# Attention scores from single-pass products of split operands, in batches of six blocks

## The chip, the cores and the metric

The kernel runs on one core of one Trainium2 chip. The metric is the time on the device in microseconds (us); lower is better. A core has a matrix engine (TensorE, PE in the profile, its weight loads PEld), VectorE (DVE), ScalarE (ACT), GpSimd (POOL) and SyncE (SP), whose queue issues most of the DMAs here. Matrix products are written to PSUM; everything else is kept in SBUF.

## The reference

The input has 4 images of 384 channels and 48 x 48 positions, so N = 2304 positions an image. There are 8 heads of 48 channels.

```python
x_flat = x.reshape(B, C, N).transpose(0, 2, 1)
local = depthwise_conv_7x7(x) * inv + shift              # batch norm folded in
x_norm = layernorm(x_flat)
q, k, v = split_heads(x_norm @ qkv_w.T + qkv_b)
q = q + split_heads(layernorm(local_flat))
attn = softmax(einsum('bhnd,bhmd->bhnm', q, k) * hd ** -0.5)
out = einsum('bhnm,bhmd->bhnd', attn, v)
out = x_flat + merge_heads(out) @ proj_w.T + proj_b
```

All of it is in float32.

## The kernel before

**Tiling.** An image is cut into 6 groups of 384 positions (`G`), 8 rows of the picture each, so there are 24 query groups, numbered `t`. Heads go in 4 pairs `p`. In the packed layout the first head of a pair has partitions 0 to 47, the second 64 to 111; the last pair's channels lie as "tails" of 16 rows at 48 to 63 and 112 to 127 of the other three, and `gather_tails` collects them by DMA into tiles of their own (`kt` for keys, `qt` for queries).

**Stages.** A start-up stage loads and scales the weights and makes keys, values and queries of image 0 (`from_x`, one call a group of positions). Then, for each of the 24 query groups, attention runs in 12 slots of 6 key blocks (a block is 128 keys), three slots a head pair. Before groups 6, 12 and 18 there is a key stage for the next image, six calls of `from_x`, each with three projections for values, keys and queries and, for the image that has just ended, the output. `both` takes one step of two such projections.

**Attention.** `score` makes the scores of a block for the two heads of a pair, transposed: keys along partitions, 384 queries along the free dimension. It issues four matmuls, each with 48 rows and 64 columns of the array: two heads by two halves of the block's keys. ScalarE then exponentiates the whole block in one instruction of 128 x 768 (L803) into a tile `pt`. `weigh` multiplies a block that is two older (`LAG`) with the values, again in four matmuls, 64 x 64 of the array: two halves of the keys by two heads. The values carry a column of ones, so that the sums of the softmax come with it. The sums stay in PSUM over all 18 blocks of a pair. `score` and `weigh` take turns on TensorE. After a pair's end `pair_out` copies one half of the sums on ScalarE and `pair_add` adds the other on VectorE.

**PSUM.** There are two pools of two slots each, `ring` for the scores and `accumulator` for the sums, every slot of two banks. Other stages take from both in turn (`two_banks`).

**VectorE's work.** The 7x7 convolution is done tap by tap on VectorE: 147 steps a group (L280, L284), each a multiply and add over about 384 elements. It runs as a stream through all groups. `plan` gives every half slot a number of steps: it has a room in us for each point (`spare`, `spare_at_keys`) and dues, by which the convolution of group t+1 must be complete (slot 8 of group 0, slot 6 of the others). `convolve` issues the share of a point. Norms (`Norm`), `local_end` and `query_end` (the queries of group t+1, in slot 10) and the division of the previous group's outputs are put at fixed slots.

**Order.** PE, DVE and ACT run in the order in which the code is written; the same holds for each DMA queue. SP's queue waits in order too, so a DMA whose data are late holds back those after it.

Of the kernel before, what the change touches and what calls it, by code (L numbers as in the profile page):

```python
# [10 lines left out]
F32 = mybir.dt.float32  # L11
AF = mybir.ActivationFunctionType
# [3 lines left out]
P = 128  # L16
# [12 lines left out]
LAG = 2  # L29
# [16 lines left out]
def unshifted_pass(  # L46
# [35 lines left out]
    ps_r = ctx.enter_context(tc.tile_pool(name="ps_r", bufs=2, space=bass.MemoryType.PSUM))  # L82
    ps_o = ctx.enter_context(tc.tile_pool(name="ps_o", bufs=2, space=bass.MemoryType.PSUM))
# [3 lines left out]
    def ring():  # L87
        return ps_r.tile([P, 2, 512], F32, tag="r", name="r")

    def accumulator():  # L90
        return ps_o.tile([P, 2, 512], F32, tag="o", name="o")


    either = cycle((accumulator, ring))

    def two_banks():
        return next(either)()
# [39 lines left out]
    natural = const.tile([P, CC, T0 + 1], F32, tag="natural", name="natural")  # L137
# [20 lines left out]
    taps_in = big.tile([P, CC, T0], F32, tag="kt0", name="taps_in")  # L158
# [28 lines left out]
    packing = big.tile([P, len(pairs), P], F32, tag="k1", name="packing")  # L187
# [14 lines left out]
    def pack():  # L202
# [21 lines left out]
    staged = [  # L224
        big.tile([P, CC, C], F32, tag=f"k{NG - 1 - i}", name=f"staged{i}") for i in range(3)
    ]
# [84 lines left out]
    def spare(t, s, half):  # L311
        b, g = divmod(t, NG)
        first, second = norm_slots(t)
        time = 3.8 - (0.7 if s % 3 == 0 and half else 0.0)
# [18 lines left out]
    def spare_at_keys(b, g, h):  # L333
        time = 4.6 - {0: 0.6, 4: 1.2}.get(h, 0.0)
        if g < later(b):
            time -= {0: 2.3, 2: 2.2, 4: 2.3}.get(h, 0.0)
        if 0 < g <= later(b):
            time -= {1: 0.4, 3: 2.6}.get(h, 0.0)
        return time - {(1, 1): 2.7, (2, 1): 1.4}.get((g, h), 0.0)
# [36 lines left out]
    class Norm:  # L376
# [37 lines left out]
        def mean_kept(self):  # L414

            m = ring()[:, 0, :G]
# [88 lines left out]
    def gather_tails(dst, src):  # L505

        for c in range(CC):
            for r in (0, 64):
                nc.sync.dma_start(
                    out=dst[r + 16 * c : r + 16 * c + 16], in_=src[r + HD : r + 64, c, :]  # L510
                )

    keys, values = {}, {}

    def from_x(b, g, before=None, ao=None):
# [3 lines left out]
        k = big.tile([P, CC, G], F32, tag=f"k{g}", name=f"k{b}_{g}")  # L519
        k3 = big.tile([P, G], F32, tag=f"kt{g}", name=f"kt{b}_{g}")  # L520

        flat = big.tile([P, NB * NH * HA + 64 - HA], F32, tag=f"v{g}", name=f"v{b}_{g}")
        v = flat[:, 0 : NB * NH * HA].rearrange("p (t h d) -> p t h d", t=NB, h=NH)
        keys[b, g], values[b, g] = (k, k3), flat
# [14 lines left out]
        def key(u, r):  # L539
            project(r[:, :G], lambda c: w_qk[:, c, 1, u, :], lambda c: src[:, c, :])  # L540
            yield
            nc.scalar.activation(
                k[:, u, :], r[:, :G], AF.Identity, bias=qkb[:, 1, u : u + 1]
            )
            if u == CC - 1:
                gather_tails(k3, k)
# [107 lines left out]
    def output_bias():  # L654

        m = ring()[:, 0, 0:CC]
# [17 lines left out]
    def query_end(t):  # L674
# [3 lines left out]
        q3 = work.tile([P, G], F32, tag="qt", name=f"qt{t}")  # L678
# [6 lines left out]

    outputs = {}

    ended = []

    def pair_out():  # L690
# [3 lines left out]
        t, p, sums = ended[0]  # L694
# [9 lines left out]
    def pair_add():  # L704

        if not ended:
            return
        t, p, sums = ended.pop()
        ao, ao3, den = outputs[t]
        dst = (ao[:, p, :] if p < CC else ao3)[0 : 64 + HA]  # L710
        nc.vector.tensor_add(dst, sums[0 : 64 + HA, 1, :G], dst)  # L711
# [34 lines left out]
    def load_residual(t, tag="xr", bufs=2):  # L746
# [13 lines left out]
    def fetch(t):  # L760
        if t < NT - NG:
            ao = work.tile([P, CC, G], F32, tag="af", name=f"af{t}")
# [21 lines left out]
    sums = None  # L784

    def score(t, p, kb):
        q, q3 = queries[t]
        k, k3 = keys[t // NG, kb // NB]
        blk = kb % NB
        r = ring()  # L790
        for j in range(2):
            rows = slice(64 * j, 64 * j + HD)
            kk, qq = (k[rows, p, :], q[rows, p, :]) if p < CC else (k3[rows], q3[rows])
            for h in halves:
                nc.tensor.matmul(  # L795
                    r[h, j, :G],
                    lhsT=kk[:, blk * P + h.start : blk * P + h.stop],
                    rhs=qq,
                    start=True,
                    stop=True,  # L800
# [4 lines left out]
        if jobs:  # L805
            jobs.popleft()()

    def weigh():
        nonlocal sums
        t, p, kb, pt = weighing.popleft()  # L810
        if kb == 0:
            sums = accumulator()
        for i, h in enumerate(halves):
            for j in range(2):
                first = (kb % NB * NH + 2 * p + j) * HA
                nc.tensor.matmul(  # L816
                    sums[halves[j], i, :G],
                    lhsT=values[t // NG, kb // NB][h, first : first + 64],
                    rhs=pt[h, j, :],
                    start=kb == 0,  # L820
                    stop=kb == KB - 1,
                )
        if kb == KB - 1:
            ended.append((t, p, sums))

    def attend(t, s, half):

        p, k0 = s // (KB // BATCH), s % (KB // BATCH) * BATCH
        n = BATCH // 2
        for kb in range(k0 + n * half, k0 + n * half + n):  # L830
            score(t, p, kb)
            if len(weighing) > LAG:
                weigh()

    def rest():
        while weighing:
            weigh()
        while jobs:
            jobs.popleft()()

# [71 lines left out]
    both(making)  # L912
    convolve_first(7)
    for g in range(1, NG):
# [28 lines left out]
        both(making)  # L943
        if not last:
            convolve_first(7)
    query_end(0)
    nc.vector.tensor_add(pb, pb, added)
    plan(n_first - (each - PE_TAPS))

    for t in range(NT):  # L950
        b, g = divmod(t, NG)
        if g == 0 and b:

            rest()
            pair_out()
            pair_add()
# [678 lines left out]
```

## Time and profile before

| | us |
|---|---|
| device time, median of 3 runs | 2856.93 |
| lowest and highest run | 2855.59, 2859.35 |
| span of the profiled execution | 2857.6 |
| TensorE busy | 2838.7 (99%) |
| VectorE busy | 2344.6 (82%) |
| ScalarE busy | 1649.5 (58%) |
| start-up, to the first score | 144.3 |
| each of three key stages | 140.4 |
| last outputs, after the last group | 41.5 |

The page gives the profiled execution as its span, first to last instruction, and the span lies within the three runs, so nothing is added to it. A page line reads: line of the code, engine, operation, tile written <- tiles read, partitions x elements, count, then busy us and mean ns of one, then the engine's idle time before it and what ended that. Matmuls that run abreast in parts of the array overlap, so their count times their mean is more than their busy time. A float32 matmul has two records here, each with a weight load of its own. In the tables of windows, each engine's busy time in a stretch is followed by its number of instructions.

### The profile page before, as it was taken

To read this page: it belongs to the slowest core of one execution; us is meant where nothing else is said; L and a number is where in the kernel's file an instruction comes from. 1 tells how busy PE (TensorE), PEld (TensorE's weight loads), DVE (VectorE), ACT (ScalarE), POOL (GpSimd) and SP (SyncE) were. 2 spreads that over 40 slices of the span, in tenths; PEclk is the share of its full clock that TensorE was granted. 3 is DMA by queue.
4 is the path that set the end of the run, shared out by engine and by line. 5 is a ranking of instruction groups with operands and counts; after the bars stand their busy time and mean duration, and the time that the engine had idled before them with its cause. 6 is when DMAs were issued, how large, how long until landed. Compare 5 with 4: busy or idle time off the path is not lost.

```text
span 2857.6 us, 70328 instructions
## 1 busy us (share of the span) xinstructions
PE 2838.7 (99%) x29558; PEld 1778.1 (62%) x29558; DVE 2344.6 (82%) x4635; ACT 1649.5 (58%) x2350; POOL 14.9 (1%) x77
## 2 busy tenths in 40 slices
PE   9999999999999999999999999999999999999999
PEld 5544444654554466666655546888875545788886
DVE  7899999999888988878888889887788787887401
ACT  4366666666226666666622666666652366666662
POOL 1000000000000000000000000000000000000000
PEclk9999999999999999999999999999999999999999
DMA  5101121112231211121132112101113211111111
GB/s 106 40 5 36 45 49 35 36 26 43 71 83 25 46 35 41 31 39 24 38 94 70 28 30 50 36 22 37 44 25 94 53 20 29 43 23 32 46 38 63
DMA packets 103433, 123.71 MB, mean 43 GB/s; under 512 B 43136, under 2 KB 89152, under 8 KB 103104
## 3 DMA queue, kind: packets, MB, share of 16 engines
q1 hardware_dynamic: 99568, 115.48, 17.0%
q8 instruction: 234, 3.83, 0.6%
q10 hardware_dynamic: 2992, 3.62, 0.4%
q14 instruction: 95, 0.78, 0.1%
q0 software_dynamic: 544, 0.01, 0.0%
HBM read 81.39 MB, written 27.03 MB: 38 GB/s over the span
## 4 chain that ended last, share of the span: by engine, by line
PE 92%; DVE 6%; DMA 0%; POOL 0%; ACT 0%; issue 0%; DVEq 0%; ACTq 0%; POOLq 0%
PE o L816 37%; PE r L795 37%; PE o L503 9%; PE r L503 9%; DVE acc L284 5%; DMA pb<-in_proj_b_dram 0%; PE r L299 0%; PE r L412 0%; ACT pt L803 0%; DVE sq L401 0%; DVE xn L681 0%; DMA parts<-part 0%; DVE sq L400 0%; POOL qk_vec L167 0%; DVE acc L672 0%
## 5 line engine op out<-in xcount | busy, mean ns | idle before, releaser
L803 ACT ACTIVATE pt<-r 128x768 f32<-128x768 f32 x1728 | 1399.6, 810 | 760.1 <-PE r L795 743.6
L284 DVE SCALAR_TENSOR_TENSOR acc<-slab,vec,acc 128x368 f32<-128x368 f32 (+6 forms) x3447 | 1756.3, 582 | 1.2
L816 PE MATMUL o<-pt,v 64*64 64x384 f32 x13824 | 1544.7, 483 | 0.0
L795 PE MATMUL r<-xn,k 48*64 48x384 f32 x10368 | 1157.8, 483 | 3.7 <-ACT pt L803 3.7
L816 PEld LDWEIGHTS o<-pt,v 64*64 64x64 f32 x13824 | 715.3, 133 | 406.7 <-issue 224.0
L795 PEld LDWEIGHTS r<-xn,k 48*64 48x64 f32 x10368 | 531.9, 133 | 316.2 <-issue 176.1
L795 PE MATMUL r<-qt,kt 48*64 48x384 f32 x3456 | 388.1, 482 | 0.1
L795 PEld LDWEIGHTS r<-qt,kt 48*64 48x64 f32 x3456 | 181.3, 133 | 99.1 <-issue 43.8
L711 DVE TENSOR_TENSOR ao<-o,ao 113x384 f32<-113x384 f32 x72 | 39.9, 554 | 194.0 <-PE r L795 176.8
L503 PE MATMUL o<-xn,w_qk 128*128 128x384 f32 x450 | 153.3, 486 | 0.0
L503 PE MATMUL r<-xn,w_qk 128*128 128x384 f32 x414 | 141.1, 486 | 0.0
L503 PEld LDWEIGHTS o<-xn,w_qk 128*128 128x128 f32 x450 | 85.5, 190 | 59.6
L503 PEld LDWEIGHTS r<-xn,w_qk 128*128 128x128 f32 x414 | 78.7, 190 | 54.8
L536 ACT COPY v<-r 128x384 f32<-128x384 f32 x42 | 18.2, 482 | 126.9 <-PE r L503 126.9
L503 PE MATMUL r<-w_v,xn 128*128 128x384 f32 x252 | 85.2, 487 | 0.0
L711 DVE TENSOR_TENSOR aot<-o,aot 113x384 f32<-113x384 f32 x24 | 13.3, 556 | 82.4 <-ACT aot L702 64.8
L503 PE MATMUL o<-af,w_o 128*128 128x384 f32 x222 | 75.0, 487 | 0.0
L400 DVE TENSOR_TENSOR sq<-sq 128x384 f32<-128x384 f32 x47 | 26.0, 554 | 57.7 <-ACT sq L395 56.2
L503 PEld LDWEIGHTS r<-w_v,xn 128*128 128x128 f32 x252 | 47.6, 190 | 34.4 <-issue 1.8
L503 PE MATMUL o<-w_v,xn 128*128 128x384 f32 x180 | 64.4, 498 | 1.3 <-ACT w_v L635 1.3
L503 PEld LDWEIGHTS o<-af,w_o 128*128 128x128 f32 x222 | 42.1, 190 | 29.2
L771 DVE SCALAR_TENSOR_TENSOR xr<-r,pb,xr 128x384 f32<-128x384 f32 x27 | 16.4, 617 | 51.8 <-ACT xn L555 41.9
(139 smaller groups left out, 1036.9 us busy)
## 6 DMA issues: line engine op xcount, KB each, us to landing
xr<-in_x_dram SPq DMA_DIRECT2D x24, 576.0 KB
slab<-in_x_dram SPq DMA_DIRECT2D x32, 378.0 KB
held<-ao SPq DMA_DIRECT2D x20, 576.0 KB
af<-held SPq DMA_DIRECT2D x20, 576.0 KB
rb<-rden SPq DMA_DIRECT2D x48, 216.0 KB
out_dram<-xr SPq DMA_DIRECT2D x54, 192.0 KB
xn<-in_x_dram SPq DMA_DIRECT2D x46, 216.0 KB
slab<-in_x_dram SPq DMA_DIRECT2D x14, 297.0 KB
```

Of the source, the lines that this page charges most:

```text
L284: nc.vector.scalar_tensor_tensor(dst, src, weight, dst, ALU.mult, ALU.add)
L400: nc.vector.tensor_add(self.buf[:, 0, :], src[:, 0, :], src[:, 1, :])
L503: nc.tensor.matmul(dst, lhsT=weights(c), rhs=src(c), start=c == 0, stop=c == CC - 1)
L536: nc.scalar.copy(v[:, blk, :, 0:HD], r[:, :C].rearrange("p (h d) -> p h d", d=HD))
L711: nc.vector.tensor_add(dst, sums[0 : 64 + HA, 1, :G], dst)
L771: nc.vector.scalar_tensor_tensor(xr[:, co, :], m, pb[:, co : co + 1], xr[:, co, :], ALU.add, ALU.add)
L795: nc.tensor.matmul(r[h, j, :G], lhsT=kk[:, blk * P + h.start : blk * P + h.stop], rhs=qq, start=True, stop=True,)
L803: nc.scalar.activation(pt, r[:, :, :G], AF.Exp, scale=SCALE)
L816: nc.tensor.matmul(sums[halves[j], i, :G], lhsT=values[t // NG, kb // NB][h, first : first + 64], rhs=pt[h, j, :], start=kb == 0, stop=kb ...
```

## The change

- The keys and queries are split into a high part, rounded on writing to `float32r`, and a low part, the remainder. Since a head has 48 rows and a half of the array 64, parts are stacked along rows: the first stationary tile has the 48 high rows of the keys and the first 16 low ones, the second the other 32 low rows twice. Three queries tiles stand against them (high; low; the rest of high and of low), and a block's scores are the sum of three matmuls a head, each 64 rows by 128 columns in `float32r`, accumulated in PSUM.
- Six blocks of scores are issued, then the six blocks of values. The values use 128 rows by 64 columns, in float32 as before. The sums are taken out of PSUM after every six blocks (`sums_out`) and added up in SBUF (`sums_add`).
- PSUM is one pool of four slots for everything.
- The split keys are written to DRAM (`keys_out`), and a pair's stacked keys are read from it (`stack_keys`, two buffers), at the beginning of the pair before. The stacked queries are made by a ScalarE copy (`high_queries`), a VectorE subtraction and DMAs within SBUF (`low_queries`), in the second slot of the pair before.
- The rooms of the plan are given new values. Start-up tiles, residuals and fetched outputs get other buffers.

The core of the diff:

```diff
+HALF = mybir.dt.float32r
-LAG = 2
...
-    ps_r = ctx.enter_context(tc.tile_pool(name="ps_r", bufs=2, space=bass.MemoryType.PSUM))
-    ps_o = ctx.enter_context(tc.tile_pool(name="ps_o", bufs=2, space=bass.MemoryType.PSUM))
+    ps = ctx.enter_context(tc.tile_pool(name="ps", bufs=4, space=bass.MemoryType.PSUM))
...
-        time = 3.8 - (0.7 if s % 3 == 0 and half else 0.0)
+        time = 3.6 - (0.0 if half else 0.6) - (0.6 if half and s % 3 == 1 else 0.0)
...
-        time = 4.6 - {0: 0.6, 4: 1.2}.get(h, 0.0)
+        time = 4.6 - {0: 0.6, 1: 0.7, 2: 1.4, 4: 1.2}.get(h, 0.0)
...
     def gather_tails(dst, src):
-        for c in range(CC):
+        for i, c in enumerate((*range(CC), 0)):
...
+    def keys_out(b, g, u, k):
+        at = slice(g * G, (g + 1) * G)
+        for j in range(2):
+            r = 64 * j
+            for head, rows, n in (
+                (2 * u + j, slice(0, HD), (r, r + HD)),
+                (6 + j, slice(16 * u, 16 * u + 16), (r + HD, r + 64)),
+            ):
+                nc.sync.dma_start(
+                    out=keys[b][head, rows, :, at], in_=k[n[0] : n[1]].bitcast(F32)
+                )
+    def stack_keys(b, p, at=slice(0, N)):
+        if at.start == 0:
+            stacks[b, p] = big.tile([P, 2, N], HALF, tag="ks", name=f"ks{b}_{p}", bufs=2)
+        dst = stacks[b, p].bitcast(F32)
+        for j in range(2):
+            r, head = 64 * j, keys[b][2 * p + j]
+            nc.sync.dma_start(out=dst[r : r + HD, 0, at], in_=head[:, 0, at])
+            nc.sync.dma_start(out=dst[r + HD : r + 64, 0, at], in_=head[0:16, 1, at])
+            for i in range(2):
+                nc.sync.dma_start(
+                    out=dst[r + 32 * i : r + 32 * i + 32, 1, at], in_=head[16:HD, 1, at]
+                )
...
-            nc.scalar.activation(
-                k[:, u, :], r[:, :G], AF.Identity, bias=qkb[:, 1, u : u + 1]
-            )
-            if u == CC - 1:
-                gather_tails(k3, k)
+            bias = qkb[:, 1, u : u + 1]
+            k = work.tile([P, 2, G], HALF, tag="pt", name=f"k{b}_{g}_{u}", bufs=5)
+            nc.scalar.activation(k[:, 0, :], r[:, :G], AF.Identity, bias=bias)
+            nc.vector.scalar_tensor_tensor(
+                k[:, 1, :], r[:, :G], bias, k[:, 0, :], ALU.add, ALU.subtract
+            )
+            keys_out(b, g, u, k)
...
+    def high_queries(t, p):
+        qs = work.tile([P, 3, G], HALF, tag="qs", name=f"qs{t}_{p}", bufs=5)
+        stacked[t, p] = qs
+        nc.scalar.copy(qs[:, 0, :], query_of(t, p))
+    def low_queries(t, p):
+        qs = stacked[t, p]
+        nc.vector.tensor_sub(qs[:, 1, :], query_of(t, p), qs[:, 0, :])
+        qs = qs.bitcast(F32)
+        for j in range(2):
+            r = 64 * j
+            if p < CC:
+                nc.sync.dma_start(out=qs[r + HD : r + 64, 0:2], in_=qs[r : r + 16, 0:2])
+            for i in range(2):
+                nc.sync.dma_start(
+                    out=qs[r + 32 * i : r + 32 * i + 32, 2], in_=qs[r + 16 : r + HD, i]
+                )
...
+    def sums_out():
...
+        t, p, i, sums = ended.pop()
+        if i:
+            part = work.tile([P, G], F32, tag="part_o", name=f"o{t}_{p}_{i}")
+            nc.scalar.copy(part[0 : 64 + HA], sums[0 : 64 + HA, 0, :G])
+            parts_of.append((t, p, i, part))
+            return
...
+    def sums_add():
...
+        nc.vector.tensor_add(dst, dst, part[0 : 64 + HA])
...
     def score(t, p, kb):
-        r = ring()
-        for j in range(2):
-            rows = slice(64 * j, 64 * j + HD)
-            kk, qq = (k[rows, p, :], q[rows, p, :]) if p < CC else (k3[rows], q3[rows])
-            for h in halves:
-                nc.tensor.matmul(r[h, j, :G],
-                    lhsT=kk[:, blk * P + h.start : blk * P + h.stop], rhs=qq, start=True, stop=True)
+        ks, qs = stacks[t // NG, p], stacked[t, p]
+        r = two_banks()
+        for i, (w, m) in enumerate(((0, 0), (0, 1), (1, 2))):
+            for j, rows in enumerate(halves):
+                nc.tensor.matmul(r[:, j, :G],
+                    lhsT=ks[rows, w, kb * P : (kb + 1) * P], rhs=qs[rows, m, :],
+                    start=i == 0, stop=i == 2)
...
-    def weigh():
-        for i, h in enumerate(halves):
-            for j in range(2):
-                nc.tensor.matmul(sums[halves[j], i, :G],
-                    lhsT=values[t // NG, kb // NB][h, first : first + 64], rhs=pt[h, j, :],
-                    start=kb == 0, stop=kb == KB - 1)
+    def weigh(i, sums):
+        for j in range(2):
+            nc.tensor.matmul(sums[halves[j], 0, :G],
+                lhsT=values[t // NG, kb // NB][:, first : first + 64], rhs=pt[:, j, :],
+                start=i == 0, stop=i == BATCH - 1)
...
                 both(making)
+                stack_keys(b, 0, slice(gk * G, (gk + 1) * G))
+                if gk == NG - 2:
+                    high_queries(t, 0)
+                if gk == NG - 1:
+                    low_queries(t, 0)
...
         for s in range(NSLOT):
-            attend(t, s, 0)
+            score_batch(t, s)
+            pair, third = divmod(s, KB // BATCH)
+            if third == 0:
+                if pair < NP - 1:
+                    stack_keys(b, pair + 1)
+                elif g < NG - 1:
+                    stack_keys(b, 0)
+            if third == 1 and pair < NP - 1:
+                high_queries(t, pair + 1)
...
                 if g < NG - 1:
                     query_end(t + 1)
+                    high_queries(t + 1, 0)
...
             convolve("slot", t, s, 0)
+            sums_add()
-            attend(t, s, 1)
...
+            weigh_batch(t, s)
             convolve("slot", t, s, 1)
+            if third == 1 and pair < NP - 1:
+                low_queries(t, pair + 1)
+            if following and s == second + 1 and g < NG - 1:
+                low_queries(t + 1, 0)
```

## The prediction

> **What bounds the kernel now.** I read the page from the top: the engines' busy time, the forty slices, then the costliest groups.
>
> ```profile
> PE 2838.7 (99%) x29558; PEld 1778.1 (62%) x29558; DVE 2344.6 (82%) x4635; ACT 1649.5 (58%) x2350; POOL 14.9 (1%) x77
> ...
> PE   9999999999999999999999999999999999999999
> ...
> DVE  7899999999888988878888889887788787887401
> ```
> TensorE is never idle, but VectorE reads 9 for the first quarter too: two engines are full there.
>
> ```profile
> L803 ACT ACTIVATE pt<-r 128x768 f32<-128x768 f32 x1728 | 1399.6, 810 | 760.1 <-PE r L795 743.6
> L284 DVE SCALAR_TENSOR_TENSOR acc<-slab,vec,acc 128x368 f32<-128x368 f32 (+6 forms) x3447 | 1756.3, 582 | 1.2
> L816 PE MATMUL o<-pt,v 64*64 64x384 f32 x13824 | 1544.7, 483 | 0.0
> L795 PE MATMUL r<-xn,k 48*64 48x384 f32 x10368 | 1157.8, 483 | 3.7 <-ACT pt L803 3.7
> ```
> There are 1728 blocks (24 query groups x 4 head pairs x 18). Scores (L795) and values (L816) have 8 records a block each; they run four abreast, so durations may not be added. The timeline gives the pace, with the change of array shape into the key stage below it:
>
> ```profile
> 1004.59 0.85 PE L795 MATMUL r<-xn,k 48*64 48x384 f32 x8
> 1005.23 0.85 PE L816 MATMUL o<-pt,v 64*64 64x384 f32 x8
> 1005.88 0.85 PE L795 MATMUL r<-xn,k 48*64 48x384 f32 x8
> ```
> ```profile
> 717.87 0.50 PE L816 MATMUL o<-pt,v 64*64 64x384 f32 x4
> 718.30 0.59 PE L503 MATMUL r<-w_v,xn 128*128 128x384 f32 x1
> ```
> A block takes 1.29 us, 0.645 for scores and as much for values; a slot of six takes 7.76. The second fence: starts 0.43 apart instead of 0.32, and the first matmul 0.10 longer than the usual 0.49, so a change of shape costs 0.15 to 0.2. Last, the windows by query group (us, then busy us of PE, PEld, DVE, ACT, POOL, clock, DMA share, GB/s):
>
> ```profile
> 144.30:246.20 101.90, 97.61 (x1141) 44.17 (x1144) 100.82 (x194) 63.06 (x85) 0.00 (x0) 0.97 0.10 19
> 246.20:343.80 97.60, 95.05 (x1156) 46.80 (x1152) 96.85 (x190) 61.22 (x83) 0.00 (x0) 0.98 0.17 41
> 343.80:437.00 93.20, 93.20 (x1156) 44.97 (x1152) 92.61 (x182) 61.53 (x83) 0.00 (x0) 1.00 0.17 40
> ...
> 717.40:857.80 140.40, 140.40 (x445) 82.29 (x440) 122.18 (x236) 34.47 (x71) 0.16 (x2) 1.00 0.29 79
> ...
> 1043.40:1136.70 93.30, 93.30 (x1158) 64.31 (x1154) 81.70 (x160) 61.52 (x83) 0.00 (x0) 1.00 0.14 35
> ```
> In the first image VectorE is 99% busy and sets the end of the first two groups; from the second image on it has 12 us of room in a group. A key stage (717 to 858) is TensorE's.
>
> **What the Trainium skill says.** "FP8 and Floating Point Precision", TensorE Precision Notes: true FP32 takes four passes (high and low parts against each other), reduced FP32 is read and truncated. The trace agrees with four passes: 1.29 us for two rounds of four is 0.162 us a pass. It shows no reduced product. "TensorEngine Tiling (Array Packing)", Key Properties: changing the tiling mode drains the engine; the trace has that at 0.15 to 0.2 us. "TensorE: Matmul & The Clock Gate", LDWEIGHTS: a load takes its columns over 1.2 GHz, whatever the rows, so an estimated 107 ns for 128 columns. The trace agrees: the first 128x128 matmul above waits 0.10 us.
>
> **The change, part by part.**
> *Scores.* A block's four 48x64 four-pass matmuls become six 64x128 single-pass ones, two row halves abreast and three deep: 3 x 0.162 = 0.485 us instead of 0.645. The unknown is the pass. Bounds: 0.162 (one column a cycle, as each pass of the four) and 0.323 (half that rate); less than a pass is excluded. I take 0.162, since a load of 0.105 fits beneath it.
> *Values.* Two 128x64 matmuls of four passes abreast instead of four 64x64: 0.645 again.
> *Batching.* Two changes of shape a slot, which today's order has none of: 0.35 us. Slot: 18 x 0.162 + 24 x 0.162 + 0.35 = 7.15 us. ScalarE starts exponentials 0.70 us apart when they queue (two in 1.51 us at 858.76), so six end about 5.2 us after the first score and the last values wait for none; of four PSUM slots, the one for the sums waits for the third exponential, within 0.1 us of the end of the scores. I take 7.2, so 86.4 us a group where TensorE rules (93.2 now).
> *ScalarE.* +192 copies of sums (0.473, L702) and 96 of queries (0.48): 137 us. It goes from 58% to about 64%, hidden under TensorE; if the exponentials' pace fell to 0.81, the sums' slot would wait 0.1 us, 29 us in all. The copy of the next group's first queries waits for VectorE's `query_end`; behind it stand the sums and slot 11's exponentials, but VectorE ends it about when slot 10's exponentials end.
> *VectorE.* Added a group: four subtractions for the low queries and four more adds of sums (8 instead of 4), at 0.56 (TENSOR_TENSOR of L401, 558 ns), 4.4 us. Added a key stage: 18 low keys at 0.61, 11 us. In the key stage (VectorE then 133 of 140 us) and from image 1 on this lies beside TensorE; without that cover each microsecond would count. The keys' PSUM is now given back by VectorE instead of ScalarE, with four slots of 3.9 us work between, so I cost that at nothing. In the first image nothing covers it.
> *First image.* VectorE's busy time of its six windows is 557.1; plus 6 x 4.4 it is 583.5; at 99%, 589 us. TensorE would need 6 x 86.4 = 518. So VectorE sets it: from about 147 (144.3, the end of start-up, and 3 for the new subtractions) to 736, where it ended at 717.4. The planner spreads the convolution by ratios of room, and the dues stay, so it moves next to nothing out of this image.
> *Queues.* SP gains per group 32 loads of keys, 22 of low rows, 2 of tails; per key stage 72 + 48 - 36. An SP issue is 0.6 us here:
>
> ```profile
> 141.77 3.69 SPq L509 DMA_DIRECT2D qt<-xn  x6
> ```
> ```profile
> 25.00:30.00 5.00, 5.00 (x17) 3.03 (x16) 5.00 (x11) 5.00 (x19) 0.00 (x0) 1.00 1.10 214
> ```
> A pair's keys are 256 rows of 9216 bytes, 2.36 MB. The full queues moved 214 GB/s: 11 us, after up to 5 of issue, and they are issued three slots (21.6 us) ahead. Hidden; past 21.6 each microsecond would be TensorE's. The low query rows are the tight wait: the scores of the next pair, and with them all of TensorE, queue behind six issues (3.6 us) and a landing of about 2 (L456 issues at 1261.40, L457, which waits for its landing, at 1263.43). VectorE is done about 5 us into the slot (0.9 for the copy of the last sums, an add, seven convolution steps at 0.51, the subtraction), and 9.4 remain to the next pair: 4 to spare inside a group. What stands behind them on SP, the denominators and the norms' parts, has a slot or more. Between groups the eight tails (4.8 us) stand ahead of them: about 1.2 us late, five times an image. At the end of a key stage SP first issues the last outputs (VectorE ends them at 859.4, TensorE could begin at 857.8), then eight key loads and six low rows, 8.4 us, then lands: 10 us of waiting. Bounds: 0 and 14 an image, 0 and 4 a group. POOL's queue gets nothing. Before the first group the same wait is hidden by VectorE's own load.
>
> *Sum* against the profiled execution (span 2857.6; the median of the runs, 2856.93, differs by 0.02%): 736, then three images of key stage 140.4 + 10 and attention 6 x 86.4 + 5 x 1.2 = 524, then the tail 41.5 as now: 736 + 3 x 674.4 + 41.5 = 2800 us, -2.0%. VectorE has 505 us in the second image (478.2 + 26.4) and less later, under 524.
>
> **Rivals.**
> *TensorE everywhere.* If convolution or other VectorE work slips past the first image's dues, or costs less: 149 (start-up with 5 of waiting) + 6 x 12 x 7.14 = 514, then 3 x (142 + 514), then 41.5: about 2670. For it: VectorE has 12 us of room later. Against: the dues are fixed, and VectorE is at 99% before the change.
> *Hand-overs.* TensorE waits at each pair, because small DMAs stand behind 2.36 MB on the same rings ("DMA: Bandwidth & Descriptors", Queues, rings and completion order: each engine consumes a ring in order; the trace has no such collision). The 72 pairs of images 1 to 3 at 0.9 us are 65 us: 2865. For it: only 4 us to spare; against: 11 of 21.6 us suffice for the keys.
> *Weights or stream, the other side.* If the two row halves' 128-column loads follow each other, a product takes 2 x 0.107 = 0.213 us; a slot 18 x 0.213 + 3.88 + 0.35 = 8.07, a group 96.8, and the whole 149 + 24 x 96.8 + 3 x 150 + 41.5 = 2964. At half the streaming rate, which also stands for "not single-pass", a slot is 10.0 and the whole about 3530. The point: 57 us over the 216 slots of images 1 to 3 are 0.264 a slot, so a product above 0.176 us decides for slower. Against: today's four loads start within one burst (8 loads in 0.50 us a round of 0.645). For: those were of 64 columns, in four separate tiles.
>
> **How the numbers follow.** Chances: forecast 0.63 (own range 2740 to 2850), TensorE everywhere 0.06, hand-overs 0.15, products over the point 0.16. A measurement of this kernel tells 0.2%, some 6 us, from no change. Faster: 0.63 + 0.06 + 0.03 of the hand-overs = 0.72. Same: 0.05, of the hand-overs. Slower: 0.07 of them + 0.16 = 0.23. The range 2725 to 2880 holds the forecast but for 0.01, the hand-overs, and 0.03 of the third rival just over its point: 0.80.
>
> **What would show it.** Score records with starts 0.162 us apart; slots of 7.2 us from the second image on; group windows of about 97 us in the first image with VectorE at 99%; some 10 us between a key stage and its first scores, ended by a DMA; VectorE with about 2490 us busy. Wrong, if score records stand over 0.176 apart, or the first image's groups take under 93 us, or long waits on key loads appear.

## The result, and the profile after

| | before | after |
|---|---|---|
| device time, median | 2858.14 us (4 runs, 2855.59 to 2859.52) | 3094.46 us (4 runs, 3089.99 to 3096.22) |
| span of the profiled execution | 2857.6 us | 3094.4 us |

The ratio of the times is 1.0824, 95% interval 1.0809 to 1.0839: the change costs 8.2%. The forecast was 2800 us, 2725 to 2880.

First the page of the kernel after, with the same rows as before and, new, the busy share of the DMA engines and of SyncE's and ScalarE's queue (packets, MB, share of 16 engines):

```profile
PE 2846.5 (92%) x19190; PEld 1786.4 (58%) x19190; DVE 2474.7 (80%) x4899; ACT 1655.1 (53%) x2638; POOL 14.9 (0%) x77
...
PE   8877898889988999898999899999999989999999
...
DVE  7779889888889788786789888878878877888612
...
DMA  6255666777645767767654677677675557767774
...
q1 hardware_dynamic: 187120, 393.98, 64.1%
```
TensorE's row of nines is gone; so is VectorE's in the first quarter. Neither engine is full any more, and no other one took their place: work waits for transfers. The DMA engines, busy 17.0% with this queue before, are at 64.1%. The groups of the same page say who waits (the last column is the idle time ahead of a group, and what ended it):

```profile
L288 DVE SCALAR_TENSOR_TENSOR acc<-slab,vec,acc 128x368 f32<-128x368 f32 (+6 forms) x3447 | 1768.5, 587 | 1.2
L864 ACT ACTIVATE pt<-r 128x768 f32<-128x768 f32 x1728 | 1259.7, 827 | 337.6 <-PE r L856 298.9
L856 PE MATMUL r<-qs,ks 64*128 64x384 f32 x10368 | 1092.9, 357 | 201.6 <-DMA qs<-qs 118.3
...
L871 PE MATMUL o<-pt,v 128*64 128x384 f32 x6912 | 1183.6, 492 | 0.0
...
L795 DVE RECIPROCAL rd<-rd 128x24 f32<-128x24 f32 x24 | 7.3, 303 | 189.3 <-DMA rd<-den 189.3
...
L470 DVE TENSOR_REDUCE few<-four 128x12 f32<-128x48 f32 x80 | 18.6, 233 | 129.7 <-DMA four<-parts 129.7
```
Two of VectorE's smallest instructions carry 319 us of its idle time: the reciprocal of the softmax sums (L795, 24 of them) and the sum of a norm's partial results (L470). In the kernel before they stood at 7.9 us and 29.9 us. TensorE's scores (L856) wait 118.3 us for the low rows of the queries (`qs<-qs`). All three wait for small DMAs.

When nothing is late, the pipeline does what the change intends. The timeline of TensorE shows one slot from score start to score start, 1805.89 to 1813.26:

```profile
1805.89 3.41 PE L856 MATMUL r<-qs,ks 64*128 64x384 f32 x36
1809.23 4.09 PE L871 MATMUL o<-pt,v 128*64 128x384 f32 x24
1813.26 0.96 PE L856 MATMUL r<-qs,ks 64*128 64x384 f32 x8
```
That is 7.37 us, and the median slot is 7.36 (3.34 from the first score to the first value, 4.02 from there to the next score), where six blocks took 7.76 before. The windows (columns as in the prediction) are of two groups of the first image, the first key stage and two groups of the second image:

```profile
306.20:415.40 109.20, 96.34 (x722) 62.51 (x720) 94.39 (x186) 62.40 (x94) 0.00 (x0) 0.91 0.65 121
415.40:521.40 106.00, 93.26 (x722) 58.99 (x720) 97.40 (x191) 61.54 (x94) 0.00 (x0) 0.97 0.67 123
833.10:1000.40 167.30, 145.48 (x451) 84.28 (x447) 147.20 (x284) 35.13 (x73) 0.33 (x4) 0.95 0.46 125
1095.80:1192.10 96.30, 91.26 (x722) 58.16 (x720) 82.98 (x164) 61.35 (x94) 0.00 (x0) 0.98 0.74 136
1286.90:1390.90 104.00, 95.46 (x724) 59.90 (x724) 83.57 (x171) 63.17 (x100) 0.00 (x0) 0.95 0.70 132
```
Twelve slots of 7.36 us are 88.3. These groups take 96 to 109 us, with TensorE and VectorE both idle for part of it. The granted clock is below 1.00 in all of them, which comes back below.

The whole by stages:

| us | before | forecast | after | after less forecast |
|---|---|---|---|---|
| start-up | 144.3 | 147 | 193.3 | 46 |
| first image | 573 | 589 | 640 | 51 |
| three key stages | 421 | 451 | 478 | 27 |
| images 2, 3, 4 | 3 x 559 | 3 x 524 | 596, 592, 553 | 169 |
| tail | 41.5 | 41.5 | 42.5 | 1 |

The last image alone is below its 559 of before; VectorE has less to do there (its last digits are 6, 1 and 2).

The chain of waits shows how a small DMA comes late (start, duration, what):

```profile
1848.53 13.51 DMA ks<-keys
1862.06 0.51 SPq L784
...
1866.42 1.85 DMA rd<-den
1868.30 0.32 DVE rd L795
```
A key load takes 13.5 us to land. Only then does SyncE issue the last of L784's DMAs, which move the sums of the last pair into the tails of the other three, and the six low-row DMAs behind it; then `rd` is loaded, which takes 1.85 us, and the reciprocal, with VectorE behind it, goes on. So this small DMA was late because it was issued late. SyncE's own waits say how often that happens (total us, times, longest us):

```profile
SPq L780 <- DMA ks<-keys: 112.6, 78, 3.0
SPq L784 <- DMA ks<-keys: 87.7, 80, 2.7
SPq L94 <- DMA ks<-keys: 60.0, 48, 3.2
```
With the smaller ones, SyncE waits 362 us for key loads to land. In the trace its 2903 DMAs signal their landing on eight semaphores in turn, some 363 on each, and an issue waits for its own semaphore, that is, for the DMA eight before it (2797 of them show this wait). Behind eight key loads the small DMAs therefore wait for key loads, whether they need the keys or not.

### The profile page after: what moved, and what is told of

Its sections match the earlier page's. It is cut to its first block, busy times and chain, and to the rows that moved or that the text cites. A ratio compares the mean times of both kernels' runs of the same rounds, so it can differ in the third digit from the quotient of the medians.

```text
span 3094.4 us, 52948 instructions
## 1 busy us (share of the span) xinstructions
PE 2846.5 (92%) x19190; PEld 1786.4 (58%) x19190; DVE 2474.7 (80%) x4899; ACT 1655.1 (53%) x2638; POOL 14.9 (0%) x77
## 3 DMA queue, kind: packets, MB, share of 16 engines
q1 hardware_dynamic: 187120, 393.98, 64.1%
## 4 chain that ended last, share of the span: by engine, by line
PE 34%; DVE 33%; DMA 22%; SPq 7%; issue 2%; ACT 1%; POOL 0%; DVEq 0%; ACTq 0%; POOLq 0%
DVE acc L288 21%; PE r L507 13%; PE o L871 11%; PE r L856 10%; DMA ks<-keys 7%; DMA four<-parts 4%; DMA xn<-in_x_dram 3%; DMA parts<-part 3%; SPq L740 3%; DMA qs<-qs 2%; SPq L738 1%; DVE sq L405 1%; DMA rd<-den 1%; DMA rden<-rd 1%; DVE sq L456 1%
## 5 line engine op out<-in xcount | busy, mean ns | idle before, releaser
L864 ACT ACTIVATE pt<-r 128x768 f32<-128x768 f32 x1728 | 1259.7, 827 | 337.6 <-PE r L856 298.9
L856 PE MATMUL r<-qs,ks 64*128 64x384 f32 x10368 | 1092.9, 357 | 201.6 <-DMA qs<-qs 118.3
L856 PEld LDWEIGHTS r<-qs,ks 64*128 64x128 f32 x10368 | 955.3, 196 | 418.7 <-issue 265.9
L871 PE MATMUL o<-pt,v 128*64 128x384 f32 x6912 | 1183.6, 492 | 0.0
L871 PEld LDWEIGHTS o<-pt,v 128*64 128x64 f32 x6912 | 472.8, 137 | 593.0 <-issue 510.6
L507 PE MATMUL r<-xn,w_qk 128*128 128x384 f32 x864 | 293.1, 498 | 0.0
L756 ACT COPY o<-o 113x384 f32<-113x384 f32 x192 | 91.7, 478 | 320.8 <-PE o L871 320.7
L507 PEld LDWEIGHTS r<-xn,w_qk 128*128 128x128 f32 x864 | 169.7, 196 | 120.7 <-issue 11.8
L795 DVE RECIPROCAL rd<-rd 128x24 f32<-128x24 f32 x24 | 7.3, 303 | 189.3 <-DMA rd<-den 189.3
L507 PE MATMUL r<-w_v,xn 128*128 128x384 f32 x432 | 147.0, 493 | 9.7 <-DVE xn L502 8.9
L507 PEld LDWEIGHTS r<-w_v,xn 128*128 128x128 f32 x432 | 82.2, 192 | 69.9 <-DVE xn L502 10.5
L470 DVE TENSOR_REDUCE few<-four 128x12 f32<-128x48 f32 x80 | 18.6, 233 | 129.7 <-DMA four<-parts 129.7
L507 PE MATMUL r<-af,w_o 128*128 128x384 f32 x360 | 119.1, 487 | 0.0
L576 DVE SCALAR_TENSOR_TENSOR k<-r,qkb,k 128x384 fp32r<-128x384 f32 x72 | 44.4, 616 | 67.8 <-ACT k L575 67.4
L507 PEld LDWEIGHTS r<-af,w_o 128*128 128x128 f32 x360 | 68.3, 190 | 47.7 <-issue 0.6
L775 DVE TENSOR_TENSOR ao<-ao,o 113x384 f32<-113x384 f32 x144 | 79.7, 554 | 18.2 <-ACT o L756 18.2
L575 ACT ACTIVATE k<-r,qkb 128x384 fp32r<-128x384 f32 x72 | 41.9, 582 | 92.4 <-PE r L507 43.3
```

The costliest lines, as they stand in the source:

```text
L507: nc.tensor.matmul(dst, lhsT=weights(c), rhs=src(c), start=c == 0, stop=c == CC - 1)
L575: nc.scalar.activation(k[:, 0, :], r[:, :G], AF.Identity, bias=bias)
L576: nc.vector.scalar_tensor_tensor(k[:, 1, :], r[:, :G], bias, k[:, 0, :], ALU.add, ALU.subtract)
L756: nc.scalar.copy(part[0 : 64 + HA], sums[0 : 64 + HA, 0, :G])
L775: nc.vector.tensor_add(dst, dst, part[0 : 64 + HA])
L856: nc.tensor.matmul(r[:, j, :G], lhsT=ks[rows, w, kb * P : (kb + 1) * P], rhs=qs[rows, m, :], start=i == 0, stop=i == 2,)
```

## The experiments

Each ratio is to the kernel before, measured beside it on the same chip, with its 95% interval. Line numbers of edited kernels move by some lines.

**Are the key loads the cause?** One sixth of them:

```diff
     def stack_keys(b, p, at=slice(0, N)):
+        if at.start:
+            return
+        at = slice(0, G)
...
-                    lhsT=ks[rows, w, kb * P : (kb + 1) * P],
+                    lhsT=ks[rows, w, kb % NB * P : (kb % NB + 1) * P],
```


> Leaves out five sixths of the key loads: each pair's stacked keys are loaded for the first 384 positions alone, and every block uses those columns. All else is as in the changed kernel. Queue theory (the key loads stand ahead of the small transfers on which VectorE and TensorE wait): the 217 us that score phases last beyond 3.33 us each fall under 60, key stages to about 145, the whole to 2830 to 2880. VectorE theory (added VectorE work in its fixed order sets the end): over 3040. Products theory (the slot itself is too long): over 3040, slots unchanged at 7.35.

Measured: 2871.43 us, 1.0045 (1.0025 to 1.0064). 223 us of the 236 are gone. The windows of this kernel, one group of the first image, one of the second, and the second key stage:

```profile
401.50:499.00 97.50, 93.14 (x720) 59.23 (x720) 96.91 (x191) 61.57 (x94) 0.00 (x0) 0.96 0.27 60
1024.30:1112.60 88.30, 88.30 (x722) 56.66 (x720) 85.00 (x168) 61.00 (x94) 0.00 (x0) 1.00 0.29 65
1465.90:1620.30 154.40, 143.54 (x453) 83.61 (x449) 141.08 (x273) 33.19 (x69) 0.33 (x4) 0.97 0.43 116
```
From the second image on TensorE is full again, at 88.3 us a group; in the first image VectorE is (96.91 of 97.50), and the image takes 587 us, where 589 were forecast. Start-up (192.0) and the second key stage (154.4, against 155.8, and not the expected 145) hardly move, so they have a cause of their own. The first key stage does move, from 167.3 to about 155.

**Is it a straight line in the bytes?** Half of the loads:

```diff
+        if at.start >= N // 2:
+            return
+        at = slice(at.start, min(at.stop, N // 2))
```


> Leaves out half of the key loads: the first 1152 positions are loaded and used for both halves of the blocks. Between a sixth (2871) and all (3094): a straight line in the bytes gives 2960; if a threshold is passed only when the rings stay full, 2890 or less.

Measured: 2894.92 us, 1.0129 (1.0099 to 1.0158). From a sixth to a half costs 24 us, from a half to the whole 200 us: not a price for each byte. SyncE's waits for key loads grow in the same way, from 0.6 to 47 and then 362 us. Where between the half and the whole the price sets in was not measured.

**Is it the burst of eight loads at a pair's start?** The same bytes, a third of them in each of the three slots:

```diff
+            piece_at = slice(third * N // 3, (third + 1) * N // 3)
+            if pair < NP - 1:
+                stack_keys(b, pair + 1, piece_at)
+            elif g < NG - 1:
+                stack_keys(b, 0, piece_at)
```


> The same bytes on the same queue, but each pair's key load is cut into three loads of 768 columns, one a slot. Burst theory (a load of 2.36 MB at once keeps the rings full for over 11 us, and small transfers wait behind it): 2920 to 3000. Volume theory (average load too high): 3070 to 3110. SyncE theory (its issues are the limit; there are 16 more a pair): over 3110.

Measured: 3128.79 us, 1.0947 (1.0915 to 1.0979). Slower still, so spreading the loads this way is no remedy. It is the SyncE theory whose range holds this: there are 24 loads a pair instead of eight, and issuing key loads takes SyncE 1091 us in this run, against 402 in the kernel after.

**Would another queue free the small DMAs?** First GpSimd's, then ScalarE's, with the four loads of `stack_keys` changed alike:

```diff
-            nc.sync.dma_start(out=dst[r : r + HD, 0, at], in_=head[:, 0, at])
+            nc.gpsimd.dma_start(out=dst[r : r + HD, 0, at], in_=head[:, 0, at])
```


> All key loads as in the changed kernel, but issued from GpSimd's queue instead of SyncE's. Queue theory, if it is the order on one queue that hurts: 2880 to 2960. If it is the sheer volume on the 16 DMA engines: over 3050. VectorE theory: 3094 within 20.

Measured: 3517.47 us, 1.2305 (1.2269 to 1.2341).

```diff
-            nc.sync.dma_start(out=dst[r : r + HD, 0, at], in_=head[:, 0, at])
+            nc.scalar.dma_start(out=dst[r : r + HD, 0, at], in_=head[:, 0, at])
```


> All key loads as in the changed kernel, but issued from ScalarE's queue, the other queue whose descriptors are made by hardware; nothing is left out. If SyncE's order and its rings make the small transfers late, 2930 to 3010, with ScalarE's issuing (8 x 0.45 us a pair) as the price. If the volume on the 16 DMA engines does it, whatever queue, 3070 or more.

Measured: 3397.0 us, 1.1885 (1.1789 to 1.1982). The timeline of ScalarE in this run shows one of the new waits, on the copy of the softmax sums:

```profile
2038.62 0.48 ACT L766 COPY ao<-o 113x384 f32<-113x384 f32 x1 [9.86 <-DMA ks<-keys]
```
While ScalarE is held at its key loads, it makes no exponentials and no copies, and TensorE waits for it (332.6 us on this copy alone). Both edits are worse than the change itself. Neither tells how the loads would do on a queue that costs nothing.

**Does one load instead of eight help, and on a queue of its own?** The stacked keys are saved to DRAM in the first group of an image, and the other five groups load each pair as one transfer of 128 rows:

```diff
+    def save_stack(b, p):
+        whole[b, p] = dram.tile([P, 2, N], F32, tag=f"whole{p}", name=f"whole{b}_{p}")
+        nc.sync.dma_start(out=whole[b, p], in_=stacks[b, p].bitcast(F32))
+
+    def load_stack(b, p):
+        stacks[b, p] = big.tile([P, 2, N], HALF, tag="ks", name=f"ks{b}_{p}", bufs=2)
+        nc.sync.dma_start(out=stacks[b, p].bitcast(F32), in_=whole[b, p])
```


> Nothing is left out. In the first group of an image the stacked keys of each pair are also written to DRAM as they lie in SBUF; from the second group on a pair's keys are one load of 128 partitions x 18432 bytes instead of eight loads of 16 to 48 rows x 9216. Same bytes, same queue. Lane theory (SyncE's DMAs go round eight completion semaphores, each issue waits for the DMA eight before it, and eight big loads take all of them): about 2900 to 2940, the first groups of images staying slow. Ring theory (small transfers queue behind 2.36 MB whatever the number of loads): 3040 or more. If the rows in few partitions made the loads slow: between, with key packets faster than 178 GB/s in all.

Measured: 2964.69 us, 1.0373 (1.0342 to 1.0403). The same with `nc.scalar.dma_start` in `load_stack`:

> As the single load, but issued from ScalarE's queue. Lane theory: about as the single load from SyncE, within 30 us, and nothing like the 3397 of eight loads from ScalarE, since one load takes one semaphore. Ring theory: 80 us or more below the single load from SyncE.

Measured: 2991.57 us, 1.0467 (1.0436 to 1.0497). More than half of the loss is gone with one load on SyncE's queue, and the other queue is a little worse: a queue of its own brings no gain here. (It has a price again: TensorE waits 54.5 us for ScalarE's copies of sums, 23.6 with SyncE's queue.) But the single load changes two things, the number of loads and their width.

**Number or width?** Two kernels, both with eight loads a pair, both from the saved array, equal in bytes and in issues. The first cuts along the free dimension (128 partitions x 2304 bytes), the second along the partitions (16 partitions x 18432 bytes):

```diff
+        for i in range(2):
+            for n in range(0, N, N // 4):
+                at = slice(n, n + N // 4)
+                nc.sync.dma_start(out=dst[:, i, at], in_=whole[b, p][:, i, at])
```


> As the single load from SyncE (2965), but cut into eight loads of 128 partitions x 2304 bytes, so that all eight semaphores are taken again while the rows still lie across all partitions. Nothing is left out. Lane theory: the gain is lost, 3040 to 3090. Width theory (loads into 16 to 48 partitions run at 151 GB/s in sum, those across 128 at 311, and the rings are full for 15.6 instead of 7.6 us): the gain stays, 2950 to 2990.

Measured: 2923.76 us, 1.0228 (1.0198 to 1.0257).

```diff
+        for r in range(0, P, 16):
+            nc.sync.dma_start(out=dst[r : r + 16], in_=whole[b, p][r : r + 16])
```


> As the eight wide loads (2924), from the same array in DRAM and with the same bytes, but each load fills 16 partitions with rows of 18432 bytes. Nothing is left out. If loads into few partitions are the cause: the load takes 14 us or more instead of 8.2, and the whole 3020 to 3090. If it was where the keys lie in DRAM (rows of 9216 bytes, 18432 apart): load about 8 us, whole 2920 to 2970.

Measured: 3455.87 us, 1.2087 (1.2052 to 1.2122). So the number of loads is not the cause, and their width is. The length of the rows is not it either: the narrow loads have the rows of 18432 bytes of the single load, which was fast. The waits of the two (total us, times, longest us), the wide one first:

```profile
DVE few L470 <- DMA four<-parts: 84.5, 28, 12.4
PE r L870 <- DMA qs<-qs: 79.9, 46, 11.6
```
```profile
PE r L868 <- DMA qs<-qs: 300.7, 135, 11.9
DVE rd L807 <- DMA rd<-den: 293.9, 22, 21.0
DVE few L470 <- DMA four<-parts: 292.9, 53, 15.6
```
The small DMAs that were late in the kernel after are later with narrow loads; with wide ones, the wait for the sums is 3.3 us instead of 189.3, ten of the 18 groups of images 2 to 4 stand at 88 to 89 us, and what is left there lies mostly at the first group of each image, whose loads are still the old ones. Both kernels have eight loads in a row ahead of the small DMAs; SyncE waits 833 us for key loads to land with narrow ones and 172 with wide ones, of which 101 are for the old loads. The records of the packets give the time of a pair's 2.36 MB, from the first packet's start to the last one's end (medians; GB/s is 2.36 MB over it):

| loads of a pair | rows each | us | GB/s | kernel's ratio |
|---|---|---|---|---|
| eight wide | 128 | 8.1 | 291 | 1.0228 |
| one | 128 | 7.6 | 310 | 1.0373 |
| the change | 16, 32, 48 | 15 | 157 | 1.0824 |
| eight narrow | 16 | 19.9 | 119 | 1.2087 |

The Trainium skill states this: "SBUF — State Buffer", the section on Door 1, the DMA port swizzle, says that a transfer's rate depends on how many of 16 ports its partitions reach, with 104 GB/s measured for partitions 0 to 15, 189 for 0 to 31, 196 for 0 to 63 and 328 for all 128. An estimate from these, with two loads of 48 rows (0.885 MB, taken at 196 since the page has no figure for 48), two of 16 (0.295 at 104) and four of 32 (1.18 at 189), is 4.5 + 2.8 + 6.2 = 13.6 us one after another; the trace has 15. For eight narrow loads it is 22.7 us, where the trace has 19.9. The page and the runs agree on the order and nearly on the size. On the two queues, the skill ("DMA: Bandwidth & Descriptors", Issuing engines are not separate DMA queues) says that all DMAs end on the same 16 engines whoever issues them; 1.0467 against 1.0373 for the single load shows no gain from a second queue.

**Start-up and key stages.** The low keys made by a second ScalarE activation instead of VectorE's subtraction:

```diff
-            nc.vector.scalar_tensor_tensor(
-                k[:, 1, :], r[:, :G], bias, k[:, 0, :], ALU.add, ALU.subtract
-            )
+            nc.scalar.activation(k[:, 1, :], r[:, :G], AF.Identity, bias=bias)
```


> The low part of the keys is written by a second ScalarE instruction instead of VectorE's subtraction (the low part is then not the remainder). VectorE theory: start-up falls from 193 to about 150, each key stage by some 12, the whole to 3000 to 3020. Queue theory: under 25 us in all, start-up still above 180.

Measured: 3059.65 us, 1.0703 (1.0672 to 1.0734). Start-up falls from 193.3 to 160.2 us, the key stages from 167, 156 and 154 to 162, 153 and 152: the VectorE theory in kind, but less than its 3000 to 3020 for the whole. The wait that goes is this one, from the waits of the kernel after within its start-up, the longest of VectorE there:

```profile
DVE k L576 <- ACT k L575: 34.9, 17, 7.2
```
VectorE's subtraction (L576) needs ScalarE's high part of the same keys (L575). While it waits in order, VectorE makes none of the norms for the next projections. The edit takes two things from VectorE at once: this wait of 34.9 us, and the subtractions themselves (18 of 0.616 us, 11 us).

The subtraction left on VectorE, but put behind the next pair of projections:

```diff
+            def low():
+                nc.vector.scalar_tensor_tensor(
+                    k[:, 1, :], r[:, :G], bias, k[:, 0, :], ALU.add, ALU.subtract
+                )
+                keys_out(b, g, u, k)
+
+            late.append(low)
```


> The changed kernel with the low keys' subtraction moved to the next pair of projections; nothing left out. If VectorE's wait for ScalarE's copy of the same keys makes start-up long: start-up 155 to 165 instead of 193, the whole about 3060. If it is the subtraction's own time: above 3085.

Measured: 3076.28 us, 1.0763 (1.0732 to 1.0794), start-up 180.5 us. A gain, but 13 us and not the 28 or more of the theory that its place in the order is all; the keys then also leave for DRAM later. How the 33 us divide between the wait and the subtractions' own time is not shown.

**The two causes together.** A sixth of the loads and the low keys on ScalarE:

> Both: a sixth of the key loads, and the low keys from ScalarE (both as described for the two single runs, with the same parts left out). If the two causes are separate, the savings of the single runs add up, to about 2790; if they cover each other, less than the sum.

Measured: 2823.87 us, 0.9878 (0.985 to 0.9907); start-up 154.8, key stages 149. The savings of the two single runs, 223 and 35 us, would make 258; together they are 271, so the causes are separate (the expected 2790 had counted on larger single savings). With both costs out of the way the change is 1.2% faster than before, and this is near the forecast.

**Does the third product matter?** A sixth of the loads, and two products of three:

```diff
-        for i, (w, m) in enumerate(((0, 0), (0, 1), (1, 2))):
+        for i, (w, m) in enumerate(((0, 0), (0, 1))):
...
-                    stop=i == 2,
+                    stop=i == 1,
```


> As the run with a sixth of the key loads, and without the third of the three products (the low rows 16 to 47 of the keys). TensorE then has 18 x 0.174 - 12 x 0.174 = 1.04 us less in a slot. If TensorE sets the pace from the second image on, groups fall from 88.3 us to where VectorE stops them, about 85, and the whole by some 60 to 90; the first image, if VectorE's, stays at about 587. If something else sets the pace, the whole stays within 15 of 2871.

Measured: 2808.47 us, 0.9826 (0.9798 to 0.9855), 63 us less than with three products. Nearly all of it is in images 2 to 4, whose groups fall from 88.3 to 85.3 us in the median. VectorE was busy for 85.0 us of such a group already, so this is where VectorE stops them, as expected. The first image stays at 586 us, against 587: TensorE has a third less score work there and the time does not move, so VectorE sets that image.

**The best version with the whole computation.** Eight wide loads and the deferred subtraction:

> Eight wide loads and the deferred low keys together, nothing left out: if the two savings add up, 2924 - 18 = 2906, still slower than the kernel before, with start-up near 185; below 2890 only if key stages gain as well.

Measured: 2901.96 us, 1.015 (1.012 to 1.0179), start-up 180.3. The gains add, and it is still slower than the kernel before.

## Why the prediction was wrong, step by step

**The step that failed** is the sentence on queues: "A pair's keys are 256 rows of 9216 bytes ... The full queues moved 214 GB/s: 11 us ... Hidden." The 214 GB/s are from a window of start-up, and they were applied to loads of 16, 32 and 48 partitions without asking what width had made that rate. These loads move 157 GB/s and take 15 us. A pair's time is three slots, 22 us, so the keys themselves still came in time (TensorE has no wait for them in its list); what did not was everything small on the same queue: the low query rows, the sums to be divided, the norms' parts. "4 to spare" for the low rows and "a slot or more" for the rest were worked out without key loads ahead of them. The term was mis-sized from nothing to 223 us (a sixth of the loads against all of them); the eight-wide kernel wins back 171 us by width alone, in five groups of six.

**The late DMAs cost twice**, and the prediction has no term for the second time. TensorE's granted clock was 0.91 to 0.98 in the late groups and 1.00 in the second-image group with a sixth of the loads. The clock's record in the kernel after has 46 stretches at half, 266 us together, and each idle time of TensorE over 2.5 us (27 of them) has one in it or just behind it. Here is the one at the end of start-up (columns as above):

```profile
183.60:197.10 13.50, 5.15 (x27) 4.30 (x29) 13.50 (x28) 2.43 (x3) 0.00 (x0) 0.50 0.48 94
```
In these stretches products start 0.320 us apart instead of 0.174. TensorE works 192 us in them over the whole, against 78 with a sixth of the loads and 13 before. In images 2 to 4 it is idle for 85 us, of which the forecast had 18, and works for 102 us at half clock, which is an estimated 50 us of lost time. With 35 us of longer slots these are some 150 of the 169 us by which the three images exceed the forecast.

**The hand-overs rival** had this mechanism, small DMAs behind 2.36 MB on the same rings, at a chance of 0.15 and 0.9 us a pair, 65 us in all. It was right in kind and wrong twice: the size, over three times as large, and the place. It priced only the low rows, where TensorE waits 118.3 us; the greater waits are VectorE's, at the division and the norms. And it had them behind the bytes on the rings, where the chain above has SyncE's issue held.

**Start-up: +3 forecast, +49 measured.** Two terms failed. "I cost that at nothing", said of the keys' PSUM that VectorE gives back, looked at the buffer and not at the order: VectorE's wait for ScalarE holds up its norms. The new subtractions of start-up were put at 3 us, though 18 of them at the prediction's own 0.61 are 11. The second activation takes 33 us of start-up away, for both together. The other term is the wait before the first group, called hidden by VectorE's own load. The timeline of TensorE at the end of start-up, with the idle time ahead of each record:

```profile
190.40 0.65 PE L856 MATMUL r<-qs,ks 64*128 64x384 f32 x1 [11.83 <-issue]
192.42 1.01 PE L856 MATMUL r<-qs,ks 64*128 64x384 f32 x4 [1.37 <-DMA qs<-qs]
```
That is 13 us in which TensorE has nothing else, while SyncE issues eight tails and then the low rows. 33 and 13 make 46 of the 49.

**Key stages.** The forecast of 10 us of waiting for SyncE's queue was right in kind: in the first one TensorE idles 11.7 us before its first score and 1.2 after it, 13 in all, within the bounds of 0 to 14. In the second and third stage it is 12.5 and 11.1 us, most of what they exceed 140.4 by (155.8 and 154.5). In the first one TensorE also waits 8.9 us for a norm of VectorE (L507 for `xn`, L502) and works 4.9 us at half clock, which is most of its further 12 us; these go with a sixth of the key loads.

**What held.** The product: starts 0.174 us apart in the median, against 0.162 forecast and 0.176 as the point of the rival on weights and stream. It stayed below the point, so that rival is not what made the change slow. (That the trace agreed with 107 ns for a load of 128 columns was read from a matmul 0.10 us longer, which was also counted to the change of shape. The records of the loads before are 190 ns for 128 columns and 133 for 64: 57 ns for 64 columns more, which does fit.) The slot: 7.36 against 7.2, which the products explain (18 x 0.012 = 0.2); over 216 slots 35 us of the 169 in images 2 to 4. What 18 products of 0.174 and 24 passes of 0.162 leave of it is 0.34 us for the two changes of shape, against 0.35. The first image: 587 us with VectorE at 97% once the loads are few, against 589, its busy time 570 instead of 583.5 and the rest small waits. VectorE over the whole: 2474.7 against 2490. (ScalarE was forecast to go from 58% to 64%; it fell to 53%, as exponentials that queue start 0.70 us apart and count with less than their 0.81.) "TensorE everywhere" is refuted by the two-product kernel, whose first image is no faster. And among the signs that would show the forecast wrong, the prediction named long waits on key loads; they appeared one step further on, in the small DMAs behind them.

**What stays open.** Why one load of 128 rows (1.0373) is slower than eight (1.0228), though its own time is shorter and SyncE waits less for it (33 us for the new loads, 71 with eight). SyncE's longest wait for a norm's part to land is 6.3 us there and 3.1 with eight, so delay on the rings is likely, but no run separates it. For the same reason the division of the 223 us between SyncE's held issue and the rings is not known; the held issue is seen, the rings are not. Why GpSimd's queue cost as much as 3517 us, which was not followed up. Why a product takes 0.174 us.

## What to carry to other kernels

A rate read from one window holds for the shape of transfer that made it: before calling a load hidden, ask how many partitions it covers, and whether a load of that width has been seen. A load that comes in time for its own reader can still be the bound, through the small DMAs behind it on its queue; list those, with the engine that waits for each and what stands behind that engine, and look at the queue's own waits too. Price a wait of TensorE with the half clock that comes with it. A producer of a second part, on a second engine that runs in order, can cost the wait for the first part, whatever the buffers allow.

## What the hardware showed that was not expected

The same 2.36 MB in the same eight DMAs took 8.1 us into 128 partitions at a time and 19.9 us into 16, and the kernel's time went from 2924 to 3456 us. Rows of 2304 bytes were no handicap against rows of 18432. The cost was far from linear in the bytes: half of them cost 24 us more than a sixth, the other half 200. And of the time that TensorE lost in images 2 to 4, the work at half clock is an estimated 50 us beside 85 us of idle time.
